# A two-layer graph network on one core: earlier weight loads, batch-norm constants per chunk, norm steps two tiles apart, and a split range check

## The chip, the cores and the metric

The kernel runs on one core of a Trainium2 chip. The metric is the device time of one execution in microseconds (us). The kernel before took 2859.97 us (median of 3 runs, 2859.72 to 2862.34).

Engines are named as in the profile: PE is the matrix engine, PEld its weight load, DVE the vector engine, ACT the scalar engine, POOL is GpSimd, SP issues the DMA transfers. SBUF and PSUM are the two memories on the chip that the kernel works in; PE's results stand in PSUM, from where DVE or ACT reads them.

## The reference, cut to what matters

```python
# x: 16 x 1024 x 256, adj: 1024 x 1024, all float32
def layer0(features, A, W1, b1, g1, be1, W2, b2, g2, be2):
    agg = einsum('nm,bmd->bnd', normalised(A), features)
    h = relu(batchnorm(agg @ W1.T + b1, g1, be1))      # statistics over all 16384 rows
    return batchnorm(h @ W2.T + b2, g2, be2)           # again over all rows

def layer1(x, para, adj, kv_w):
    c = mean(x, channels)                              # per node
    A_s = 1 - abs(2 * sigmoid(c_j - c_i) - 1)          # simplified here
    g = relu(einsum('bcn,bnm->bcm', x.T, adj * A_s) * para)   # the queries
    k, v = split(x @ kv_w)
    return softmax_attention(g, k, v, heads=4)

x = layernorm(x + layer0(x, adj, ...))
x = layernorm(x + layer1(x, para, adj, kv_w))
```

Two points of the reference make seams. Each batch norm needs the statistics of every row before its first output exists. And layer 1 works batch by batch, so its first batch has nothing to overlap with but the end of layer 0.

## The kernel before

The kernel has three parts: layer 0 up to the hidden layer (`pa`, `ph` in the profile), the second half of layer 0 (`po`, in 32 units of 512 rows), and layer 1, a pipeline of 16 batches with 16 steps each. Every step issues score matmuls (`s`), exponentials (`e`), attention matmuls (`o`), and whatever tasks a table puts into it. A chunk is 128 of the channels of a layer: the hidden layer has four (`f`), `po` has two (`c`). A pass is one PE instruction of the profile; one with 512 columns takes 0.43 us from start to start.

```python
        def bn_affine(st, n, g, be, bias, s, t, add_bias, name):
            mv = w0.tile([P, n, 2], F32, name=f"mv_{name}")
            for c in range(n):
                nc.vector.bn_aggr(mv[:, c, :], st[:, c].rearrange("p k s -> p (k s)"))
            # ... six more small DVE operations, and the root on GpSimd, over all n chunks at once
        # ... hidden layer: ACT copies ph, DVE takes its statistics
        bn_affine(st1, HT, g1t, be1t, b1t, s1, t1, True, "bn1")

            def second(u):
                # ...
                for c in range(CT):
                    p = ps.tile([P, FB], F32, tag="a", name="po")
                    for k in range(HT):
                        nc.tensor.matmul(
                            p, W2T[:, k, ts(c, P)], hT[u][:, k, :], start=(k == 0), stop=(k == HT - 1)
                        )
                    nc.vector.tensor_scalar(y[:, c, :], p, b2t[:, c : c + 1], None, op0=OP.add)
                    nc.vector.bn_stats(st2[:, c, b * NH + h, :], y[:, c, :])
                nc.sync.dma_start(yT_dram[b][:, :, ts(h, FB)], y)
        # ...
        bn_affine(st2, CT, g2t, be2t, None, s2, t2, False, "bn2")
```

The tasks of layer 1 that matter here: `load` fetches a tile of 128 rows, `bn2` applies the second batch norm to it, `ln1_a` transposes it (`py`), adds x and takes statistics, `ln1_b` applies the layer norm and sums the row, `x1_t` transposes the result (`px`), `crow` scales the row means `cs` and spreads them over partitions (`pc`), `wg_a` and `wg_b` make the graph weights, `graph` makes the queries (`pg`, then two DVE operations on `qT`), `finish_a` and `finish_b` end a tile.

```python
        def bn2(b, j):
            for c in range(CT):
                t = yts[b, j][:, c, :]
                nc.vector.tensor_scalar(t, t, s2[:, c : c + 1], t2[:, c : c + 1], op0=OP.mult, op1=OP.add)
        def ln1_b(b, j):
            r = x1s[b, j]
            ln_apply(r, r, *mvs.pop((b, j)))                 # DVE, waits for GpSimd's root
            nc.vector.tensor_reduce(css[b][:, j : j + 1], r, AX.X, OP.add)
        def crow(b):
            nc.vector.tensor_scalar_mul(css[b], css[b], 1.0 / C)
            # ... eight transposes of css into PSUM (pc), two ACT copies
        # ...
            for j in range(NT):
                put(b - 2, 3 + j, load, b, j)
                put(b - 2, 4 + j, bn2, b, j)
                put(b - 2, 5 + j, ln1_a, b, j)
                put(b - 2, 6 + j, ln1_b, b, j)
                put(b - 2, 7 + j, x1_t, b, j)
            put(b - 2, 7 + NT, crow, b)
        # ...
            if g == load_weights_at:       # in the first step that loads a tile, after its task list
                load_weights()             # kvw, adj, para: 5.5 MB, on the same queue as the tiles
    fast()
    # then: a range check of all softmax sums, whose flag can start a slow general version
```

## Time and profile before

| view | number |
|---|---|
| span of the profiled run | 2855.9 us |
| PE busy | 2751.3 us (96%) |
| DVE, ACT, POOL busy | 53%, 41%, 13% |
| one batch of layer 1 | 115.08 us |
| last `po` to first `pk` (start to start) | 46.7 us |
| last `o` matmul to the end | 23.5 us |

The main views of this profile stand in the prediction below. One more is the timeline of the tail. Its columns are start, duration, engine, source line, operation, output and inputs, then in brackets the engine's idle time just before it and who ended it.

```profile
2835.43 0.18 DVE L518 RECIPROCAL RD<-pf 128x4 f32<-128x4 f32 x1 [2.16 <-PE pf L516]
2838.53 0.17 DVE L518 RECIPROCAL RD<-pf 128x4 f32<-128x4 f32 x1
...
2849.92 0.14 DVE L606 TENSOR_SCALAR badi<-bad 1x1 int32<-1x1 f32 x1
```

Each of the last four tiles starts with a reciprocal, and these stand 3.1 us apart. The flag of the range check (`badi`) is ready 14.6 us after the first of them.

### The profile page before, as it was taken

How to read it: one execution, taken by the hardware profiler on the slowest of the kernel's cores; microseconds unless marked ns; L12 is line 12 of the kernel's file. 1: busy time of each engine (PE TensorE's matmuls, PEld its weight loads, DVE VectorE, ACT ScalarE, POOL GpSimd, SP SyncE). 2: the span in 40 equal slices, each digit the busy share in tenths (PEclk: the TensorE clock that was granted, in tenths of full speed). 3: DMA queues.
4: the chain of work that ended last, by engine and by line, in shares of the span. 5: the costliest groups of instructions: out<-in, count | busy, mean ns of one | idle time of the engine just before them, and what ended most of it. 6: DMA issues, size and time to landing. Idle time of an engine off the chain costs nothing.

```text
span 2855.9 us, 25725 instructions
## 1 busy us (share of the span) xinstructions
PE 2751.3 (96%) x9426; PEld 1170.7 (41%) x9426; DVE 1502.2 (53%) x2717; ACT 1162.0 (41%) x1487; POOL 377.5 (13%) x523
## 2 busy tenths in 40 slices
PE   7999999999899599999999999999999999999997
PEld 5444444444344244434434344344343443434332
DVE  3011111012444457667686686776766857668556
ACT  1111111112741155645546455364464553644633
POOL 0000000000000112122121221221212212113012
PEclk7999999999999699999999999999999999999998
DMA  3121122120463410001010010010100100101000
GB/s 104 59 88 59 74 88 78 70 103 0 158 232 111 151 30 25 28 19 39 19 32 30 16 43 24 23 35 18 38 30 15 41 20 29 34 13 43 8 10 22
DMA packets 109988, 146.97 MB, mean 51 GB/s; under 512 B 10272, under 2 KB 92704, under 8 KB 103712
## 3 DMA queue, kind: packets, MB, share of 16 engines
q1 hardware_dynamic: 109856, 145.27, 14.9%
q8 instruction: 76, 1.25, 0.2%
q14 instruction: 56, 0.46, 0.1%
HBM read 86.52 MB, written 58.72 MB: 51 GB/s over the span
## 4 chain that ended last, share of the span: by engine, by line
PE 96%; DVE 2%; DMA 1%; POOL 0%; ACT 0%; issue 0%; SPq 0%; POOLq 0%; ACTq 0%
PE s L455 17%; PE o L485 17%; PE pg L435 16%; PE pa L201 15%; PE po L264 8%; PE ph L214 8%; PE pk L408 4%; PE pv L419 4%; PE pf L515 2%; PE pd L504 1%; PE py L364 1%; PE px L377 1%; PE pd L172 1%; PE pc L388 1%; PE pf L516 0%; DMA yt<-yT 0%
## 5 line engine op out<-in xcount | busy, mean ns | idle before, releaser
L467 ACT ACTIVATE e<-s 128x1024 f32<-128x1024 f32 x512 | 496.5, 1022 | 480.7 <-PE s L455 479.4
L455 PE MATMUL s<-qT,kT 64*128 64x512 f32 x2048 | 508.7, 615 | 0.0
L485 PE MATMUL o<-e,v 128*64 128x512 f32 x2048 | 495.7, 605 | 0.0
L476 DVE TENSOR_TENSOR acc<-acc,e 128x1024 f32<-128x1024 f32 x384 | 468.7, 1221 | 41.7 <-ACT e L467 27.8
L435 PE MATMUL pg<-wg,x 128*128 128x512 f32 x1024 | 477.2, 604 | 0.2 <-ACT x1T L378 0.2
L201 PE MATMUL pa<-AhT,x 128*128 128x512 f32 x1024 | 441.9, 592 | 0.0
L233 DVE BATCH_NORM_STATS2 st<-ph 128x6 f32<-128x512 f32 x128 | 89.4, 699 | 570.4 <-ACT hT L232 570.4
L455 PEld LDWEIGHTS s<-qT,kT 64*128 64x128 f32 x2048 | 176.2, 186 | 327.0 <-issue 286.8
L201 PEld LDWEIGHTS pa<-AhT,x 128*128 128x128 f32 x1024 | 194.5, 190 | 244.4 <-issue 244.2
L435 PEld LDWEIGHTS pg<-wg,x 128*128 128x128 f32 x1024 | 182.2, 190 | 240.3 <-issue 219.8
L400 DVE SCALAR_TENSOR_TENSOR wg<-wg,adj_sb 128x1024 f32<-128x1024 f32 x128 | 156.8, 1225 | 227.2 <-ACT wg L396 227.2
L214 PE MATMUL ph<-agg,W1T 128*128 128x512 f32 x512 | 222.2, 592 | 0.0
L485 PEld LDWEIGHTS o<-e,v 128*64 128x64 f32 x2048 | 124.3, 136 | 225.4 <-issue 212.5
L208 ACT COPY agg<-pa 128x512 f32<-128x512 f32 x64 | 37.5, 586 | 402.3 <-PE pa L201 402.3
L68 POOL TENSOR_TENSOR rs_a<-rs_a,mhalf 128x1 f32<-128x1 f32 x128 | 195.9, 1530 | 10.6
L378 ACT COPY x1T<-px 128x256 f32<-128x256 f32 x128 | 47.4, 370 | 357.5 <-PE px L377 357.5
L66 POOL TENSOR_SCALAR rs_z<-mv_z 128x1 f32<-128x1 f32 x128 | 40.8, 319 | 1000.2 <-DVE mv_z L313 1000.2
L264 PE MATMUL po<-hL,W2T 128*128 128x512 f32 x384 | 165.0, 592 | 0.0
L214 PEld LDWEIGHTS ph<-agg,W1T 128*128 128x128 f32 x512 | 97.3, 190 | 122.5 <-issue 122.5
L395 ACT ACTIVATE wg<-crow,cs 128x1024 f32<-128x1024 f32 x128 | 147.0, 1149 | 0.0
L396 ACT ACTIVATE wg<-wg 128x1024 f32<-128x1024 f32 x128 | 135.3, 1057 | 4.1
L232 ACT COPY hT<-ph 128x512 f32<-128x512 f32 x128 | 75.0, 586 | 144.7 <-PE ph L214 144.7
(97 smaller groups left out, 2229.5 us busy)
## 6 DMA issues: line engine op xcount, KB each, us to landing
h<-hT SPq DMA_DIRECT2D x24, 1024.0 KB, 3.8
hL<-h SPq DMA_DIRECT2D x24, 1024.0 KB, 6.2
x<-in_x_dram SPq DMA_DIRECT2D x16, 1024.0 KB, 5.5
yT<-y SPq DMA_DIRECT2D x32, 512.0 KB, 3.6
yt<-yT SPq DMA_DIRECT2D x128, 128.0 KB, 2.6
xr<-in_x_dram SPq DMA_DIRECT2D x128, 128.0 KB, 2.3
out_dram<-r SPq DMA_DIRECT2D x128, 128.0 KB, 1.7
A<-in_adj_dram SPq DMA_DIRECT2D x4, 1024.0 KB, 8.1
```

Of the source, the lines that this page charges most:

```text
L68: nc.gpsimd.tensor_tensor(dst, src, mhalf[:, :n], OP.pow)
L201: nc.tensor.matmul(p, xts[b][:, k, ts(c, P)], AhT[:, k, ts(h, FB)], start=(k == 0), stop=(k == NT - 1),)
L214: nc.tensor.matmul(p, W1T[:, k, ts(f, P)], aggT[b][:, k, ts(h, FB)], start=(k == 0), stop=(k == CT - 1),)
L264: nc.tensor.matmul(p, W2T[:, k, ts(c, P)], hT[u][:, k, :], start=(k == 0), stop=(k == HT - 1))
L395: nc.scalar.activation(t, crows[b], AF.Abs, bias=css[b][:, i : i + 1], scale=-1.0)
L396: nc.scalar.activation(t, t, AF.Tanh, scale=-0.5)
L400: nc.vector.scalar_tensor_tensor(t, t, 1.0, adj_sb[:, i, :], op0=OP.add, op1=OP.mult)
L435: nc.tensor.matmul(pg[b], x1s[b, k][:, ts(c, P)], wgs[b, k][:, ts(h, FB)], start=(k == 0), stop=(k == NT - 1))
L455: nc.tensor.matmul(t[:, h, :], kTs[b, pair][h * HD : (h + 1) * HD, ts(cb, P)], qTs[b, pair][h * HD : (h + 1) * HD, ts(hf, FB)], start=True ...
L467: nc.scalar.activation(E[g, a], S.pop((g, a)), AF.Exp)
L476: nc.vector.tensor_add(ACC[b, hf, pair], ACC[b, hf, pair], E[g, a])
L485: nc.tensor.matmul(O[b, hf, pair][h * HD : (h + 1) * HD, :], vs[b][:, cb, pair * P + h * HD : pair * P + (h + 1) * HD], E[g, a][:, h, :], ...
```

## The change

The intent is to shorten the places where PE stands idle: the two seams of layer 0, the short wait in each batch, and the tail. The diff, cut to its core (left out, among other things: `reuse_waits="tile"` for the PSUM buffers of `po`, more small buffers in layer 1, and `finish_b` of the last four tiles one step later):

```diff
-        def bn_affine(st, n, g, be, bias, s, t, add_bias, name):
+        def bn_affine(st, c, g, be, bias, s, t, name):          # one chunk c
+            nc.vector.bn_aggr(mv, st[:, c].rearrange("p k s -> p (k s)"))
+            rsqrt(rs, mv[:, 1:2], EPS)                          # GpSimd
+            nc.vector.tensor_add(mu, mv[:, 0:1], bias[:, col])
+            nc.vector.tensor_sub(mu, bias[:, col], mu)
+            nc.vector.tensor_mul(s[:, col], rs, g[:, col])
+            nc.vector.scalar_tensor_tensor(t[:, col], mu, s[:, col], be[:, col], op0=OP.mult, op1=OP.add)
@@ hidden layer, after each chunk's statistics
+                            if u == len(units) - 1:
+                                bn_affine(st1, f, g1t, be1t, b1t, s1, t1, "bn1")
@@ second(u)
+                if u == order[0]:
+                    mm.sort(key=lambda ck: ck[1])               # by chunk of the hidden layer
-                    nc.vector.tensor_scalar(y[:, c, :], p, b2t[:, c : c + 1], None, op0=OP.add)
-                    nc.vector.bn_stats(st2[:, c, b * NH + h, :], y[:, c, :])
+                    nc.vector.bn_stats(st2[:, c, b * NH + h, :], po[c])
+                    nc.scalar.copy(y[:, c, :], po[c])
+                    if u == order[-1]:
+                        bn_affine(st2, c, g2t, be2t, b2t, s2, t2, "bn2")
@@ loop over the units (the buffers of layer 1 now lie on the right side of SBUF)
+                if k == KEEP:
+                    load_weights()
+                if k == len(units) - 2:
+                    for j in range(LDP):
+                        load(0, j)
@@ layer 1
-                nc.vector.tensor_scalar(t, t, s2[:, c : c + 1], t2[:, c : c + 1], op0=OP.mult, op1=OP.add)
+                nc.scalar.activation(t, t, AF.Identity, bias=t2[:, c : c + 1], scale=s2[:, c : c + 1])
@@ ln1_b: apply and row sum in one DVE operation
-            ln_apply(r, r, *mvs.pop((b, j)))
-            nc.vector.tensor_reduce(css[b][:, j : j + 1], r, AX.X, OP.add)
+            nc.vector.scalar_tensor_tensor(r, r, mv[:, 0:1], rs.to_broadcast([P, C]),
+                op0=OP.subtract, op1=OP.mult, accum_out=css[b][:, j : j + 1])
@@ wg_a, for odd i
+                nc.scalar.activation(t, crows[b], AF.Tanh, bias=hcs[b][:, i : i + 1], scale=-0.5)
+                nc.vector.tensor_scalar(ti, ti, -(2**31), None, op0=OP.bitwise_or)
@@ finish_b, on ACT, with a product from GpSimd
-            ln_apply(r, r, *mr)
+            nc.scalar.activation(r, r, AF.Identity, bias=nm, scale=rs)
@@ the table
-                put(b - 2, 6 + j, ln1_b, b, j)
-                put(b - 2, 7 + j, x1_t, b, j)
+                put(b - 2, 7 + j, ln1_b, b, j)
+                put(b - 2, 8 + j, x1_t, b, j)
+        put(B - 1, NS // NH, range_so_far)          # the first 120 of 128 tiles
+        put(B - 1, NS + FB // P, range_all)         # the last 8, right after their reciprocals
```

More of the change, by code (lines that the diff above doesn't have):

```diff
@@ L79, in gnn_norm_attention_kernel @@
     yT_dram = [yT_all[b] for b in range(B)]
+    LDP = 3
     s2 = const.tile([P, CT], F32, name="s2")
@@ L96, in gnn_norm_attention_kernel @@
         aggT = []
-        def bn_affine(st, n, g, be, bias, s, t, add_bias, name):
-            mv = w0.tile([P, n, 2], F32, name=f"mv_{name}")
-            for c in range(n):
-                nc.vector.bn_aggr(mv[:, c, :], st[:, c].rearrange("p k s -> p (k s)"))
-            mu = w0.tile([P, n], F32, name=f"mu_{name}")
-            if add_bias:
-                nc.vector.tensor_add(mu, mv[:, :, 0], bias)
-                nc.vector.tensor_sub(mu, bias, mu)
-            else:
-                nc.vector.tensor_scalar_mul(mu, mv[:, :, 0], -1.0)
-            var = w0.tile([P, n], F32, name=f"var_{name}")
-            nc.vector.tensor_copy(var, mv[:, :, 1])
-            rs = w0.tile([P, n], F32, name=f"rs_{name}")
-            rsqrt(rs, var, EPS)
-            nc.vector.tensor_mul(s, rs, g)
-            nc.vector.tensor_mul(mu, mu, s)
-            nc.vector.tensor_add(t, mu, be)
+        def bn_affine(st, c, g, be, bias, s, t, name):
+            col = slice(c, c + 1)
+            mv = w0.tile([P, 2], F32, name=f"mv_{name}{c}")
+            nc.vector.bn_aggr(mv, st[:, c].rearrange("p k s -> p (k s)"))
+            rs = w0.tile([P, 1], F32, name=f"rs_{name}{c}")
+            rsqrt(rs, mv[:, 1:2], EPS)
+            mu = w0.tile([P, 1], F32, name=f"mu_{name}{c}")
+            nc.vector.tensor_add(mu, mv[:, 0:1], bias[:, col])
+            nc.vector.tensor_sub(mu, bias[:, col], mu)
+            nc.vector.tensor_mul(s[:, col], rs, g[:, col])
+            nc.vector.scalar_tensor_tensor(t[:, col], mu, s[:, col], be[:, col], op0=OP.mult, op1=OP.add)
+        s1 = w0.tile([P, HT], F32, name="s1")
+        t1 = w0.tile([P, HT], F32, name="t1")
         with ExitStack() as ph1:
@@ L233, in gnn_norm_attention_kernel, with load_weights, load @@
                             nc.vector.bn_stats(st1[:, f, u, :], p)
+                            if u == len(units) - 1:
+                                bn_affine(st1, f, g1t, be1t, b1t, s1, t1, "bn1")
                         if u < len(units) - KEEP:
                             nc.sync.dma_start(h_dram[u], hT.pop(u))
-        s1 = w0.tile([P, HT], F32, name="s1")
-        t1 = w0.tile([P, HT], F32, name="t1")
-        bn_affine(st1, HT, g1t, be1t, b1t, s1, t1, True, "bn1")
+        right = lambda name, bufs: ctx.enter_context(tc.tile_pool(name=name, bufs=bufs, side="right"))
+        keep = right("keep", 1)
+        ldp = right("ldp", LDP)
+        RD = keep.tile([P, B * NT + 1, HEADS], F32, name="RD")
+        ones32 = keep.tile([P, 32], F32, name="ones32")
+        nc.gpsimd.memset(ones32, 1.0)
+        kvw = keep.tile([P, CT, 2 * C], F32, name="kvw")
+        para_sb = keep.tile([P, CT, N], F32, name="para_sb")
+        adj_sb = keep.tile([P, NT, N], F32, name="adj_sb")
+        yts, xrs = {}, {}
+        def load_weights():
+            nc.sync.dma_start(kvw, kv_w.rearrange("(c p) f -> p c f", p=P))
+            for i in range(0, NT, 2):
+                nc.sync.dma_start(
+                    adj_sb[:, i : i + 2, :], adj[i * P : (i + 2) * P, :].rearrange("(c p) m -> p c m", p=P)
+                )
+            nc.sync.dma_start(para_sb, para.rearrange("o (c p) h w -> p c (o h w)", p=P))
+        def load(b, j):
+            yts[b, j] = ldp.tile([P, CT, P], F32, tag="yt", name=f"yt{b}_{j}")
+            nc.sync.dma_start(yts[b, j], yT_dram[b][:, :, ts(j, P)])
+            xrs[b, j] = ldp.tile([P, C], F32, tag="xr", name=f"xr{b}_{j}")
+            nc.sync.dma_start(xrs[b, j], x[b, ts(j, P), :])
         with ExitStack() as ph2:
             yp = ph2.enter_context(tc.tile_pool(name="yp", bufs=3))
-            ps = ph2.enter_context(tc.tile_pool(name="ps2", bufs=4, space=PSUM))
+            ps = ph2.enter_context(tc.tile_pool(name="ps2", bufs=4, space=PSUM, reuse_waits="tile"))
             order = list(range(len(units) - KEEP, len(units))) + list(range(len(units) - KEEP))
@@ L260, in second @@
                 y = yp.tile([P, CT, FB], F32, tag="y", name=f"y{u}")
-                for c in range(CT):
-                    p = ps.tile([P, FB], F32, tag="a", name="po")
-                    for k in range(HT):
-                        nc.tensor.matmul(
-                            p, W2T[:, k, ts(c, P)], hT[u][:, k, :], start=(k == 0), stop=(k == HT - 1)
-                        )
-                    nc.vector.tensor_scalar(y[:, c, :], p, b2t[:, c : c + 1], None, op0=OP.add)
-                    nc.vector.bn_stats(st2[:, c, b * NH + h, :], y[:, c, :])
+                po = [ps.tile([P, FB], F32, tag="a", name="po") for c in range(CT)]
+                mm = [(c, k) for c in range(CT) for k in range(HT)]
+                if u == order[0]:
+                    mm.sort(key=lambda ck: ck[1])
+                for c, k in mm:
+                    nc.tensor.matmul(
+                        po[c], W2T[:, k, ts(c, P)], hT[u][:, k, :], start=(k == 0), stop=(k == HT - 1)
+                    )
+                for c in range(CT):
+                    nc.vector.bn_stats(st2[:, c, b * NH + h, :], po[c])
+                    nc.scalar.copy(y[:, c, :], po[c])
+                    if u == order[-1]:
+                        bn_affine(st2, c, g2t, be2t, b2t, s2, t2, "bn2")
                 nc.sync.dma_start(yT_dram[b][:, :, ts(h, FB)], y)
@@ L281, in gnn_norm_attention_kernel @@
                         fetch(order[KEEP + AHEAD + k - 1])
-        bn_affine(st2, CT, g2t, be2t, None, s2, t2, False, "bn2")
+                if k == KEEP:
[3 more added lines that the diff above has]
+                        load(0, j)
     NP = HEADS // 2
     den_lo, den_hi = 1e-20, 1e30
-    keep = ctx.enter_context(tc.tile_pool(name="keep", bufs=1))
-    RD = keep.tile([P, B * NT, HEADS], F32, name="RD")
-    ones32 = keep.tile([P, 32], F32, name="ones32")
-    nc.vector.memset(ones32, 1.0)
-    ones64 = None
-    kvw = keep.tile([P, CT, 2 * C], F32, name="kvw")
-    para_sb = keep.tile([P, CT, N], F32, name="para_sb")
-    adj_sb = keep.tile([P, NT, N], F32, name="adj_sb")
-    def load_weights():
-        nc.sync.dma_start(kvw, kv_w.rearrange("(c p) f -> p c f", p=P))
-        for i in range(0, NT, 2):
-            nc.sync.dma_start(
-                adj_sb[:, i : i + 2, :], adj[i * P : (i + 2) * P, :].rearrange("(c p) m -> p c m", p=P)
-            )
-        nc.sync.dma_start(para_sb, para.rearrange("o (c p) h w -> p c (o h w)", p=P))
     def ln_stats(sm, r, name):
@@ L323, in fast @@
         pool = lambda name, bufs, **k: fx.enter_context(tc.tile_pool(name=name, bufs=bufs, **k))
-        ldp = pool("ldp", 3)
         x1p = pool("x1p", 21)
@@ L334, in fast @@
         otp = pool("otp", 3)
-        sm = pool("sm", 4)
+        sm = pool("sm", 6)
         rp = pool("rp", 4)
@@ L339, in fast @@
         ps_t = pool("ps_t", 3, space=PSUM)
-        yts, xrs, x1s, x1Ts, css, crows, mvs, wgs = {}, {}, {}, {}, {}, {}, {}, {}
+        x1s, x1Ts, css, crows, mvs, wgs = {}, {}, {}, {}, {}, {}
         kTs, qTs, vs, S, E, ACC, O, OT, DT = {}, {}, {}, {}, {}, {}, {}, {}, {}
-        pg = {}
-        def load(b, j):
-            yts[b, j] = ldp.tile([P, CT, P], F32, tag="yt", name=f"yt{b}_{j}")
-            nc.sync.dma_start(yts[b, j], yT_dram[b][:, :, ts(j, P)])
-            xrs[b, j] = ldp.tile([P, C], F32, tag="xr", name=f"xr{b}_{j}")
-            nc.sync.dma_start(xrs[b, j], x[b, ts(j, P), :])
+        pg, hcs = {}, {}
         def bn2(b, j):
@@ L370, in ln1_b @@
             r = x1s[b, j]
-            ln_apply(r, r, *mvs.pop((b, j)))
-            nc.vector.tensor_reduce(css[b][:, j : j + 1], r, AX.X, OP.add)
+            mv, rs = mvs.pop((b, j))
+            nc.vector.scalar_tensor_tensor(
+                r,
+                r,
+                mv[:, 0:1],
+                rs.to_broadcast([P, C]),
+                op0=OP.subtract,
+                op1=OP.mult,
+                accum_out=css[b][:, j : j + 1],
+            )
         def x1_t(b, j):
@@ L382, in crow @@
             nc.vector.tensor_scalar_mul(css[b], css[b], 1.0 / C)
+            hcs[b] = sm.tile([P, NT], F32, tag="hcs", name=f"hcs_{b}")
+            nc.vector.tensor_scalar_mul(hcs[b], css[b], 0.5)
             crows[b] = crp.tile([P, N], F32, tag="crow", name=f"crow_{b}")
@@ L394, in wg_a @@
             wgs[b, i] = t
-            nc.scalar.activation(t, crows[b], AF.Abs, bias=css[b][:, i : i + 1], scale=-1.0)
-            nc.scalar.activation(t, t, AF.Tanh, scale=-0.5)
+            if i % 2:
+                nc.scalar.activation(t, crows[b], AF.Tanh, bias=hcs[b][:, i : i + 1], scale=-0.5)
+                ti = t.bitcast(mybir.dt.int32)
+                nc.vector.tensor_scalar(ti, ti, -(2**31), None, op0=OP.bitwise_or)
+            else:
+                nc.scalar.activation(t, crows[b], AF.Abs, bias=css[b][:, i : i + 1], scale=-1.0)
+                nc.scalar.activation(t, t, AF.Tanh, scale=-0.5)
         def wg_b(b, i):
@@ L525, in finish_a, with range_so_far, range_all @@
             nc.vector.tensor_add(r, r, x1s.pop((b, i)))
-            R[b, i] = (r, ln_stats(sm, r, f"z{b}_{i}"))
+            mv, rs = ln_stats(sm, r, f"z{b}_{i}")
+            nm = sm.tile([P, 1], F32, tag="nm", name=f"nm_{b}_{i}")
+            nc.gpsimd.tensor_scalar(nm, mv[:, 0:1], rs, -1.0, op0=OP.mult, op1=OP.mult)
+            R[b, i] = (r, rs, nm)
         def finish_b(b, i):
-            r, mr = R.pop((b, i))
-            ln_apply(r, r, *mr)
+            r, rs, nm = R.pop((b, i))
+            nc.scalar.activation(r, r, AF.Identity, bias=nm, scale=rs)
             nc.sync.dma_start(out[b, ts(i, P), :], r)
+        last = (B - 1) * NT
+        def range_so_far():
+            flat = RD[:, :last, :].rearrange("p a h -> p (a h)")
+            for k, op in enumerate((OP.max, OP.max, OP.min, OP.min)):
+                if k % 2 == 0:
+                    nc.vector.tensor_reduce(RD[:, B * NT, k : k + 1], flat, AX.X, op)
+                else:
+                    nc.vector.tensor_copy(RD[:, B * NT, k : k + 1], RD[:, B * NT, k - 1 : k])
+        badi = []
+        def range_all():
+            flat = RD[:, last:, :].rearrange("p a h -> p (a h)")
+            mm = sm.tile([P, 4], F32, tag="mm", bufs=1, name="mm")
+            nc.vector.tensor_reduce(mm[:, 0:1], flat, AX.X, OP.max)
+            nc.vector.tensor_reduce(mm[:, 1:2], flat, AX.X, OP.min)
+            nc.vector.tensor_scalar(mm[:, 2:3], mm[:, 0:1], 1.0 / den_lo, None, op0=OP.is_le)
+            nc.vector.tensor_scalar(mm[:, 3:4], mm[:, 1:2], 1.0 / den_hi, None, op0=OP.is_ge)
+            pf = ps_t.tile([P, FB], F32, tag="t", name="pflag")
+            nc.tensor.matmul(pf[:1, :2], ones, mm[:, 2:4], start=True, stop=True)
+            bad = sm.tile([1, 2], F32, tag="bad", bufs=1, name="bad")
+            nc.vector.tensor_scalar(bad, pf[:1, :2], -1.0, float(P), op0=OP.mult, op1=OP.add)
+            badi.append(keep.tile([1, 1], mybir.dt.int32, name="badi"))
+            nc.vector.tensor_add(badi[0], bad[:, 0:1], bad[:, 1:2])
         NS = NT // 2 * NP * NH
@@ L543, in fast @@
             for j in range(NT):
-                put(b - 2, 3 + j, load, b, j)
+                if b > 0 or j >= LDP:
+                    put(b - 2, 3 + j, load, b, j)
                 put(b - 2, 4 + j, bn2, b, j)
                 put(b - 2, 5 + j, ln1_a, b, j)
-                put(b - 2, 6 + j, ln1_b, b, j)
-                put(b - 2, 7 + j, x1_t, b, j)
+                put(b - 2, 7 + j, ln1_b, b, j)
+                put(b - 2, 8 + j, x1_t, b, j)
             put(b - 2, 7 + NT, crow, b)
@@ L568, in fast @@
                 put(b, s + 1 + i % (FB // P), finish_a, b, i)
-                put(b, s + 2 + i % (FB // P), finish_b, b, i)
-        last = max(at)
+                put(b, s + 2 + i % (FB // P) + (b == B - 1 and hf == NH - 1), finish_b, b, i)
+        put(B - 1, NS // NH, range_so_far)
+        put(B - 1, NS + FB // P, range_all)
         nsteps = B * NS
-        load_weights_at = -2 * NS + 3
-        for g in range(min(at), max(last, nsteps - 1) + 1):
+        for g in range(min(at), max(max(at), nsteps - 1) + 1):
             if 0 <= g + 1 < nsteps:
@@ L581, in fast @@
                 f(*a)
-            if g == load_weights_at:
-                load_weights()
             if 0 <= g < nsteps:
                 attend(g)
-    fast()
-    with ExitStack() as cx:
-        sm = cx.enter_context(tc.tile_pool(name="smc", bufs=1))
-        psc = cx.enter_context(tc.tile_pool(name="psc", bufs=1, space=PSUM))
-        flat = RD.rearrange("p a h -> p (a h)")
-        mm = sm.tile([P, 4], F32, name="mm")
-        nc.vector.tensor_reduce(mm[:, 0:1], flat, AX.X, OP.max)
-        nc.vector.tensor_reduce(mm[:, 1:2], flat, AX.X, OP.min)
-        nc.vector.tensor_scalar(mm[:, 2:3], mm[:, 0:1], 1.0 / den_lo, None, op0=OP.is_le)
-        nc.vector.tensor_scalar(mm[:, 3:4], mm[:, 1:2], 1.0 / den_hi, None, op0=OP.is_ge)
-        pf = psc.tile([1, 2], F32, name="pflag")
-        nc.tensor.matmul(pf, ones, mm[:, 2:4], start=True, stop=True)
-        fl = sm.tile([1, 2], F32, name="fl")
-        nc.vector.tensor_copy(fl, pf)
-        bad = sm.tile([1, 1], F32, name="bad")
-        nc.vector.tensor_add(bad, fl[:, 0:1], fl[:, 1:2])
-        badi = sm.tile([1, 1], mybir.dt.int32, name="badi")
-        nc.vector.tensor_scalar(badi, bad, -1.0, 2.0 * P, op0=OP.mult, op1=OP.add)
-        flag = nc.values_load(badi[0:1, 0:1], min_val=0, max_val=2 * P, skip_runtime_bounds_check_because="a count of up to 256")
+        return nc.values_load(
+            badi[0][0:1, 0:1],
+            min_val=0,
+            max_val=2 * P,
+            skip_runtime_bounds_check_because="a count of up to 256",
+        )
+    flag = fast()
     def general(b):
```

## The prediction

> **What bounds the kernel now.** I read the page first: the busy shares, the slices, the chain of work that ended last.
>
> ```profile
> PE   7999999999899599999999999999999999999997
> PEclk7999999999999699999999999999999999999998
> PE 96%; DVE 2%; DMA 1%; POOL 0%; ACT 0%; issue 0%; SPq 0%; POOLq 0%; ACTq 0%
> ```
>
> TensorE (PE) is the bound: 96% of the chain, nines in nearly all slices (one slice is 2855.9/40 = 71.4 us). The holes are slice 1 (start), 11 (714 to 785 us, the seam between the two halves of layer 0), 14 (928 to 1000 us, the seam between the layers) and 40 (tail). The change removes no matmul, so all it can win is PE idle time: 2855.9 - 2751.3 busy = 104.6 us. The view of waits, for PE, says who holds it; columns are total us, times, longest us.
>
> ```profile
> PE py L364 <- DVE yt L355: 26.0, 6, 16.3
> PE pc L388 <- DVE cs L382: 20.0, 15, 1.4
> PE pw L161 <- DMA w1n<-in_L_gnn_W_dram: 15.1, 1, 15.1
> PE pflag L600 <- DVE mm L598: 12.6, 1, 12.6
> PE po L264 <- ACT hT L254: 8.4, 1, 8.4
> PE px L377 <- DVE x L319: 5.4, 7, 2.1
> PE py L364 <- ACT wg L395: 3.2, 1, 3.2
> ```
>
> The w1n wait is the start, which the change leaves alone. The others are four places: seam A (8.4), seam B (26.0 + 5.4 + 3.2), one 1.3 us wait in each later batch (20.0), the tail (12.6 and what follows). A gain of 2% is 57 us, over half of all idle PE time. I then read the timeline at each place.
>
> ```profile
> 717.55 0.59 ACT L232 COPY hT<-ph 128x512 f32<-128x512 f32 x1 [1.13 <-PE ph L214]
> 718.17 0.70 DVE L233 BATCH_NORM_STATS2 st<-ph 128x6 f32<-128x512 f32 x1 [1.02 <-ACT hT L232]
> 718.79 3.65 DVE L103 BATCH_NORM_AGGREGATE mv_bn<-st 128x2 f32<-128x192 f32 x4
> 725.04 20.54 ACT L254 ACTIVATE hT<-hT,t,s 128x512 f32<-128x512 f32 x29 [6.90 <-DVE t L116]
> ...
> 953.39 2.16 SPq L303 DMA_DIRECT2D adj_sb<-in_adj_dram  x4
> 955.60 0.56 SPq L306 DMA_DIRECT2D para_sb<-in_L_gnn_para_dram  x1
> 970.09 0.60 DVE L355 TENSOR_SCALAR yt<-yt,s,t 128x128 f32<-128x128 f32 x2 [14.79 <-DMA yt<-yT]
> 993.69 7.96 PE L408 MATMUL pk<-x1T,kvw 128*128 128x512 f32 x16
> ...
> 1850.94 0.16 DVE L382 TENSOR_SCALAR cs<-cs 128x8 f32<-128x8 f32 x1
> 1851.15 1.09 PE L388 MATMUL pc<-ident,cs 128*128 128x128 f32 x8 [1.32 <-DVE cs L382]
> ```
>
> Columns: start, duration, engine, instruction, then the idle time before it and its releaser. Seam A: PE ends at 717.5 and waits while DVE aggregates four chunks in a row and GpSimd takes the root. Seam B: the weights of layer 1 are issued ahead of the second tile's load, whose normalisation waits 14.79 us; then eight tiles go through at 2.87 us each (971 to 991 us), and the first large matmul (pk) starts 46.2 us after layer 0 ended (947.5). Steady batch: after the last pg matmul PE waits 1.32 us for DVE.
>
> **What the Trainium skill says.** "TensorE: Matmul & The Clock Gate", Part 1, says the array falls to half rate after an idle window of about 3.4 us and recovers after as much sustained work. The trace agrees: after the 8.39 us gap the first weight loads stand 0.86 us apart, later ones 0.43; so a gap that shrinks can also win some 1.7 us of slow matmuls. "PSUM — Partial Sum Buffer", "PSUM bank collisions raise a hardware error", has two engines' accesses to one bank serialised, reads included: above, the statistics start 0.03 us after ACT's copy ended, so both readers of a result run in turn. "ScalarE: Activation LUTs", "Table sets", puts identity, relu and abs into every set, and exp with tanh into one; the trace has one table load in the run (1.3 us), and I expect no more. "DMA: Bandwidth & Descriptors", anatomy section, gives a fixed cost of about 2.0 us to each transfer; here a 128 KB tile takes 2.6 us to land.
>
> **The change part by part.**
>
> Seam A (constants per chunk). DVE's serial work per chunk is now statistics 0.70 + aggregate 0.91 + a GpSimd round trip (gaps 0.2, 0.23, root of one column 0.57: about 1.0) + two small steps 0.4 = 3.05 us. The first statistics of the last unit are at about 713.0, so chunk 3 is ready at 713.0 + 4 x 3.05 = 725.2, no earlier than the 724.94 of before; DVE waiting for GpSimd in order eats the overlap. But chunks 0 to 2 are ready at 716, 719 and 722, and the first unit's matmuls are sorted by chunk, so three quarters of that unit is done while chunk 3 is made. Its activation (0.80) and last 4 matmuls (0.43 each) end near 727.8; before, the unit ended at 734.7. At full clock that is 7 us, with those four cold 5. **I take 6.**
>
> The y half of layer 0. DVE loses the 0.75 us bias addition, ACT gains two PSUM copies of 0.59 per unit. A unit is 16 matmuls x 0.43 = 6.86 us of PE; ACT has 4 activations (2.93 together) plus 1.2. ACT can no longer run ten units ahead, but needs only one. No effect.
>
> Weights early. 5.5 MB took some 16 us of DMA in seam B (953 to 970). They now go after unit 8, where DMA is 67 to 70% busy, PE-paced, and h tiles are fetched up to 12 units ahead; hidden. Tiles 0 to 2 of layer 1 are also loaded before the seam.
>
> Seam B, from the end T of the last po matmul: statistics, one aggregate, GpSimd and two steps end at T+3.2 (chunk 0 done before), the normalisation is now two ACT instructions, py and the addition follow: first addition at T+4.3 (before T+6.7). Then tiles at DVE's pace: addition 0.45 + statistics 0.46 + aggregate 0.18 + one fused apply-and-sum 0.46 with its accumulator read 0.08, about 1.6 us, with no GpSimd wait as the second step comes two tiles later. A load ring of 3 buffers gives (2.6 + 0.7 + 0.9)/3 = 1.4, so DVE still sets it. The eighth addition is at T+15.5, its apply at T+17.6, and pk 2.6 us later (before 2.95, less the reduction): T+20.2. **26 us saved.** In the next stretch ACT bound the wg tiles (1.15 + 1.06 us each, 8 of them); four lose an instruction, but two bn2 activations per tile now stand in ACT's queue too. The first py of batch 1 comes about 17.3 after pk instead of 18.05, the eighth wg tile 1.7 earlier. **I take 1.5.**
>
> Steady batches. 115.0 us each, PE busy 113.75. The x1 transposes (0.38 us of PE) move one step later, between the last pg matmul and pc: they fill 0.38 of the 1.32. The chain pg, two DVE operations, cs is otherwise unchanged. 15 x 0.38 = **5.7 us**. DVE sheds bn2 (16 x 0.29), the reduction (8 x 0.42) and the final apply (8 x 0.41), and gains four integer ORs; ACT gains about what it loses. DVE was 80 and ACT 59 of 115 us, so neither matters.
>
> Tail. Before: four tiles at 3.1 us each, because DVE waits for GpSimd, then 2.2 us of range check over 512 numbers, then 5.8 us to the end of the span. After: 1.76 us per tile (no wait, the apply on ACT), then a check over 36 numbers of 1.4 us. 4 x 1.34 + 0.8 = **6 us**, if the 5.8 us follows the flag and not the last store, which now ends about 2 us after it.
>
> Sum: 6 + 26 + 1.5 + 5.7 + 6 = 45.2 us; 2860 - 45 = about 2814 us.
>
> **Rivals.** (1) ACT becomes the seam's bound: bn2 and wg share its queue in order. Against: 0.7 us of bn2 plus a 0.37 copy per tile is under 1.6. If it held, seam B would give 20, the time 2820. (2) The weights or the y stores fall behind: y has 3 buffers, 20.6 us of room, and a store queued behind 5.5 MB waits some 16 to 19 us. If that stalled PE once, 5 us lost. (3) The 1.3 us wait per batch goes wholly, if DVE gets there earlier: 14 us more, 2800. Against: in the trace DVE idles 6.7 us before the two qT operations, so PE, not DVE load, times that chain. (4) The transfers of the seam were hidden anyway: no, the 14.79 us wait has PE idle 16.3.
>
> **Range and chances.** Largest uncertainties: tile pace (1.4 to 2.1 us, 5 us in all), seam A's clock (2), the tail (2), new waits in 15 batches (each 0.1 us is 1.5). I give 2804 to 2826. Over 2% needs 57 us, 12 beyond my sum, with rival 3 or all parts at their best: 0.1. Slower over 2%: 0.01.
>
> **What would show it.** Right: no wait of DVE for a yt load at the seam, pk about 20 us after the last po; tiles there 1.6 us apart; the pc wait 0.94 x 15 = 14 us; tail from last o matmul to the end 17 us instead of 23; batches 114.6 us long; a first unit of seam A ending 10 us after the last ph. Wrong: PE waits on ACT yt in every batch, a second table load, po waiting on hL or y, or pc waits near zero.

## The result, and the profile after

The changed kernel took 2817.44 us (median of 4 runs, 2816.89 to 2818.15), the kernel before on the same chip 2861.15 us (4 runs). The ratio is 0.9847 (95% interval 0.983 to 0.9864). A ratio here is the mean time of one kernel's fast runs over that of the other's of the same rounds, so it isn't quite the ratio of the medians. A change of less than 2% is called "same" here, as was forecast, and 2817 lies in the forecast range.

The busy share of PE in 40 slices, and the PE waits of the changed kernel (total us, times, longest us):

```profile
PE   7999999999999899999999999999999999999998
```

```profile
PE pc L405 <- DVE cs L397: 18.0, 15, 1.2
PE pflag L580 <- DVE mm L578: 6.2, 1, 6.2
PE py L371 <- ACT yt L362: 5.4, 3, 2.0
PE px L392 <- DVE x L379: 3.7, 7, 1.1
PE po L288 <- ACT hT L276: 3.2, 3, 1.4
```

The hole at slice 11 is closed, that at slice 14 is shallow. The 26.0 us wait for a normalised tile is 5.4 us, the wait at the first seam 3.2 instead of 8.4, the tail's 6.2 instead of 12.6. The wait before `pc` has hardly moved: 18.0 instead of 20.0 us.

To see where the time went I cut both traces at the same instructions, from start to start (the starts are read to 0.1 us, so a difference can be off by 0.1):

| stretch | before | after | gained | predicted |
|---|---|---|---|---|
| start to first `pa` | 58.2 | 62.4 | -4.2 | 0 |
| first `pa` to last `ph` | 658.7 | 658.7 | 0 | 0 |
| last `ph` to last `po` (seam A) | 230.1 | 223.8 | 6.3 | 6 |
| last `po` to first `pk` (seam B) | 46.7 | 19.4 | 27.3 | 26 |
| first `pk` to first `s` | 49.8 | 47.7 | 2.1 | 1.5 |
| first `s` to last `o` (batches) | 1788.9 | 1786.8 | 2.1 | 5.7 |
| last `o` to the end (tail) | 23.5 | 17.6 | 5.9 | 6 |
| sum without the start | 2797.7 | 2754.0 | 43.7 | 45.2 |

The start is not the change's; that is shown in the first experiment. Without it the traces differ by 43.7 us. That the medians differ by 43.7 us too is partly chance, as each timed run has an early or a late start.

**Seam A** in the timeline of the changed kernel:

```profile
722.25 0.81 ACT L276 ACTIVATE hT<-hT,t,s 128x512 f32<-128x512 f32 x1
...
729.42 0.22 DVE L111 SCALAR_TENSOR_TENSOR t<-mu_bn,s,be1t 128x1 f32<-128x1 f32 x1
730.60 14.86 PE L288 MATMUL po<-hT,W2T 128*128 128x512 f32 x34 [1.09 <-ACT hT L276]
```

Chunk 0 is activated at 722.25, 0.5 us after the last `ph` matmul ended (721.7). The last chunk's constants are ready at 729.6. Four passes of 0.43 us later, at 732.3, the first unit is done: 10.6 us after the last `ph`, against 17.2 before.

**Seam B**, two successive tiles of the kernel before, then the changed kernel:

```profile
974.28 0.41 DVE L366 TENSOR_TENSOR x<-py,xr 128x256 f32<-128x256 f32 x1
977.15 0.41 DVE L366 TENSOR_TENSOR x<-py,xr 128x256 f32<-128x256 f32 x1
```

```profile
945.49 0.70 DVE L292 BATCH_NORM_STATS2 st<-po 128x6 f32<-128x512 f32 x1 [0.27 <-PE po L288]
949.60 0.42 DVE L373 TENSOR_TENSOR x<-py,xr 128x256 f32<-128x256 f32 x1 [0.94 <-PE py L371]
...
956.02 0.18 DVE L327 BATCH_NORM_AGGREGATE mv_a<-st_a 128x2 f32<-128x6 f32 x1
956.12 0.45 DVE L379 SCALAR_TENSOR_TENSOR x<-x,mv_a,rs_a 128x256 f32<-128x256 f32 x1
956.49 0.09 DVE L379 DVE_READ_ACCUMULATOR x<-x,mv_a,rs_a 128x1 f32 x1
956.49 0.42 DVE L373 TENSOR_TENSOR x<-py,xr 128x256 f32<-128x256 f32 x1
...
959.28 0.42 DVE L373 TENSOR_TENSOR x<-py,xr 128x256 f32<-128x256 f32 x1
964.32 8.20 PE L431 MATMUL pk<-x1T,kvw 128*128 128x512 f32 x16
```

Layer 0 ends at 945.45. The first addition of layer 1 comes 4.15 us later, the eighth 9.7 us after that, so a tile takes 1.38 us (before: 2.87). The first `pk` starts 18.9 us after the end of layer 0, against 46.1.

**One batch**: two pairs of transposes in a stream, then the work around `pc`:

```profile
1002.90 0.38 PE L392 MATMUL px<-ident,x 128*128 128x128 f32 x2
1003.12 0.38 PE L371 MATMUL py<-ident,yt 128*128 128x128 f32 x2
...
1817.07 0.38 PE L392 MATMUL px<-ident,x 128*128 128x128 f32 x2
1818.34 0.16 DVE L397 TENSOR_SCALAR cs<-cs 128x8 f32<-128x8 f32 x1
1818.65 1.06 PE L405 MATMUL pc<-ident,cs 128*128 128x128 f32 x8 [1.20 <-DVE cs L397]
```

The transposes do stand in the gap now, but PE still waits 1.20 us, where the prediction had 0.94.

**The tail**:

```profile
2801.41 0.18 DVE L541 RECIPROCAL RD<-pf 128x4 f32<-128x4 f32 x1 [2.79 <-PE pf L539]
2803.18 0.15 DVE L541 RECIPROCAL RD<-pf 128x4 f32<-128x4 f32 x1
...
2809.38 0.15 DVE L584 TENSOR_TENSOR badi<-bad 1x1 int32<-1x1 f32 x1
```

The tiles come 1.75 us apart and the flag is ready 8.1 us after the first reciprocal. From the flag to the end of the span it is 6.9 us (before: 5.8), so in this pair one microsecond of the gain was given back. The last tile's apply on ACT starts only at 2809.89, after the flag; that this is the reason is argued, not shown, as the stretch lies between 6.1 and 7.1 us in the other profiles with this apply.

### The profile page after: what moved, and what is told of

It is laid out like the page before. It is cut to its first block, busy times and chain, and to the rows that moved or that the text cites. A ratio compares the mean times of both kernels' runs of the same rounds, so it can differ in the third digit from the quotient of the medians.

```text
span 2816.4 us, 26243 instructions
## 1 busy us (share of the span) xinstructions
PE 2750.9 (98%) x9426; PEld 1174.2 (42%) x9426; DVE 1352.6 (48%) x2364; ACT 1295.2 (46%) x1871; POOL 498.2 (18%) x660
## 4 chain that ended last, share of the span: by engine, by line
PE 96%; DVE 2%; DMA 0%; ACT 0%; issue 0%; POOL 0%; SPq 0%; DVEq 0%; POOLq 0%; ACTq 0%
PE s L478 17%; PE o L508 17%; PE pg L458 16%; PE pa L199 16%; PE po L288 8%; PE ph L212 8%; PE pk L431 4%; PE pv L442 4%; PE pf L538 2%; PE pd L527 1%; PE py L371 1%; PE pd L170 1%; PE px L392 1%; PE pc L405 1%; PE pf L539 0%; DMA w1n<-in_L_gnn_W_dram 0%
## 5 line engine op out<-in xcount | busy, mean ns | idle before, releaser
L66 POOL TENSOR_SCALAR rs_z<-mv_z 128x1 f32<-128x1 f32 x128 | 52.2, 408 | 900.3 <-DVE mv_z L327 884.4
L66 POOL TENSOR_SCALAR rs_a<-mv_a 128x1 f32<-128x1 f32 x128 | 124.8, 975 | 435.8 <-DVE mv_a L327 435.7
L68 POOL TENSOR_TENSOR rs_a<-rs_a,mhalf 128x1 f32<-128x1 f32 x128 | 157.9, 1234 | 10.7
L393 ACT COPY x1T<-px 128x256 f32<-128x256 f32 x128 | 47.7, 372 | 239.9 <-PE px L392 239.9
```

Of the source, the lines that this page charges most:

```text
L66: nc.gpsimd.tensor_scalar(dst, src, add, None, op0=OP.add)
L68: nc.gpsimd.tensor_tensor(dst, src, mhalf[:, :n], OP.pow)
```

## The experiments

Twelve kernels ran, all correct. Their times scatter by 4 to 5 us for a reason that has nothing to do with them (the first experiment), so beside each median I give the span of the profiled run less its start. It agrees to 0.2 us in the two profiles of the kernel before. Seam A (223.7) and the batches (1786.7) repeat to 0.1 us in every kernel that doesn't touch them. Seam B (19.4 to 20.2), the stretch from `pk` to `s` (47.1 to 48.2) and the tail (17.0 to 18.0) scatter by about 1 us, so a smaller difference there is not read as the edit's.

| run | median us | ratio to before | span less start | seam A | seam B | pk to s | batches | tail |
|---|---|---|---|---|---|---|---|---|
| before | 2861.15 | 1 | 2797.7 | 230.1 | 46.7 | 49.8 | 1788.9 | 23.5 |
| changed | 2817.44 | 0.9847 | 2754.0 | 223.8 | 19.4 | 47.7 | 1786.8 | 17.6 |
| e9_before_again | 2859.57 | 0.9998 | 2797.9 | 230.0 | 46.6 | 49.7 | 1789.0 | 23.8 |
| e1_weights_alone | 2845.06 | 0.9947 | 2783.7 | 230.0 | 32.4 | 50.1 | 1788.9 | 23.5 |
| e2_weights_late | 2832.04 | 0.9897 | 2768.2 | 223.7 | 33.8 | 47.2 | 1786.7 | 18.0 |
| e3_one_apart | 2827.26 | 0.9883 | 2767.7 | 223.7 | 27.3 | 51.3 | 1788.8 | 17.8 |
| e4_scale_early | 2797.43 | 0.9778 | 2736.8 | 223.7 | 19.8 | 47.5 | 1769.6 | 17.4 |
| e5_constants_whole | 2825.00 | 0.9873 | 2763.0 | 230.3 | 21.6 | 48.2 | 1786.7 | 17.4 |
| e6_no_sort | 2819.68 | 0.9859 | 2758.3 | 228.2 | 19.6 | 47.1 | 1786.8 | 17.8 |
| e7_bn2_on_dve | 2822.14 | 0.9868 | 2759.8 | 223.7 | 25.2 | 48.4 | 1786.7 | 17.0 |
| e8_tail_dve | 2820.40 | 0.9861 | 2758.3 | 223.7 | 20.2 | 47.4 | 1786.7 | 21.5 |
| e11_wg_two_steps | 2816.54 | 0.9845 | 2756.3 | 223.7 | 19.9 | 49.3 | 1786.7 | 17.9 |
| e12_hcs_gpsimd | 2814.16 | 0.9840 | 2754.0 | 223.7 | 20.0 | 47.5 | 1786.7 | 17.3 |
| e10_best | 2795.86 | 0.9778 | 2735.3 | 221.5 | 19.7 | 48.1 | 1769.5 | 17.7 |

### e9_before_again: is the later start the change's?

The edit is none: the kernel before, once more.

> The kernel before, unchanged, to see how much of the 4.2 us later start of the changed kernel's profile is the run's own. Theory (the clock of the 128 one-column matmuls at the start differs from run to run): the first aggregation matmul may start near 58 us or near 62 us, and the span less that start is 2797.7 +- 1 us again. Rival (the change made the start slower): 58.2 us again here, and 62.4 us in every kernel derived from the changed one. Time 2860 +- 3 us.

Its own profile again had the early start. But the kernels derived from the changed one, whose start is untouched, fell on both sides. Here the start's 128 one-column matmuls in the changed kernel, and in e12_hcs_gpsimd:

```profile
18.70 27.31 PE L170 MATMUL pd<-ones,A 128*128 128x1 f32 x128
```

```profile
18.59 24.21 PE L170 MATMUL pd<-ones,A 128*128 128x1 f32 x128
```

Of fourteen profiles ten took 24.2 to 24.4 us and four 27.3 us (the changed kernel, e2, e4, e5). So the rival falls: it is the run's own, and the profiles before and after happened to fall on different sides. The timed runs of the kernel before show two levels too. The mean clock that the profiler reports as granted to PE tells the side: in this run 2857.74 and 2857.45 us came with 0.982, 2861.50 and 2861.40 us with 0.987. All four runs of the changed kernel have 0.995, the clock of its late start, so its median is that of the slower side, and a median of a derived kernel can lie some microseconds below it for that reason alone. What decides the side stays open.

### e1_weights_alone and e2_weights_late: were the transfers of the seam hidden?

e1 is the kernel before with this part alone, e2 the changed kernel without it:

```diff
# e1, on the kernel before           # e2, on the changed kernel
+                if k == KEEP:        -                if k == KEEP:
+                    load_weights()   -                    load_weights()
+                if k == len(units) - 2:
+                    for j in range(3):     + if g == 4 - 2 * NS:   # after tile 0's bn2
+                        load(0, j)         +     load_weights()
```

> Kernel before plus only the early weights and the three early tile loads. Theory: the 16.3 us PE wait for the second tile falls under 2 us, the seam from the last po matmul to the first pk matmul goes from 46.1 to about 31 us, the second half of layer 0 keeps its 230 us, time 2860 - 15 = 2845 us. Rival (the transfer only moves its cost: h tiles or y stores stall in layer 0, or the tiles are slow for another reason): po waits on hL or ACT appear, or the seam stays over 40 us; time over 2853 us.

> Changed kernel with the weights issued after layer 0 again, but behind the three early tile loads. Theory: the 5.5 MB take 16 us of DMA from about T (end of the last po matmul), tile 3 lands near T+18 instead of T+7, so the seam grows from 18.9 to about 31 us and the time from 2817 to 2829 us. Rival (three early tiles alone cover the transfer): seam under 22 us, time under 2821 us.

The longest PE waits for a normalised tile, in e1 and in e2:

```profile
PE py L370 <- DVE yt L361: 11.9, 7, 5.7
```

```profile
PE py L369 <- ACT yt L360: 19.1, 4, 13.7
```

Alone, the early weights gave 14.0 us (2797.7 to 2783.7), all of it in seam B; layer 0 kept its 230.0 us. Taken out of the changed kernel they cost 14.2 us, two more than expected, and a 13.7 us wait is back. So the transfer was not hidden before, it is hidden now, and three early tiles don't cover it. In e1 the tiles still come 2.87 us apart: that half of the seam belongs to other parts.

### e3_one_apart: the two norm steps of a tile

```diff
-                put(b - 2, 7 + j, ln1_b, b, j)
-                put(b - 2, 8 + j, x1_t, b, j)
+                put(b - 2, 6 + j, ln1_b, b, j)
+                put(b - 2, 7 + j, x1_t, b, j)
```

> Changed kernel with the two norm steps of a tile one step apart again (apply at 6+j, transposes at 7+j). Theory: at the seam DVE waits for GpSimd in each tile again, so tiles come about 1.9 to 2.0 us apart instead of 1.39 (+4 us), and the batches return from 114.92 to 115.08 us (+2.3 us in all, pc wait from 18 to 20 us): time 2817 + 6 = 2823 us. Rival (tile pace set by the load ring or by ACT): pace stays 1.4, time 2819 to 2820 us.

It cost 13.7 us, more than twice what I expected (the medians say 9.8, the changed kernel's being that of the late start). Two successive applies on DVE at the seam:

```profile
952.37 0.48 DVE L379 SCALAR_TENSOR_TENSOR x<-x,mv_a,rs_a 128x256 f32<-128x256 f32 x1 [0.99 <-POOL rs_a L68]
...
954.87 0.48 DVE L379 SCALAR_TENSOR_TENSOR x<-x,mv_a,rs_a 128x256 f32<-128x256 f32 x1 [0.99 <-POOL rs_a L68]
```

Tiles come 2.50 us apart: DVE's work of 1.4 us and the whole round trip to GpSimd, 0.99 us, of which I had counted half. That is 7.9 us in seam B. Another 3.6 us came in the next stretch: PE waited 2.06 us for a graph weight instead of 1.27 and then ran six `pg` passes in 4.54 us instead of 2.84; the recorded clock is 0.50 over most of them, and 1.00 there in the changed kernel. The batches lost 2.0 us, and their `pc` wait was 20.0 again: the distance between the steps is what the batches had gained.

### e7_bn2_on_dve: which engine sets the pace of the seam?

```diff
-                nc.scalar.activation(t, t, AF.Identity, bias=t2[:, c : c + 1], scale=s2[:, c : c + 1])
+                nc.vector.tensor_scalar(t, t, s2[:, c : c + 1], t2[:, c : c + 1], op0=OP.mult, op1=OP.add)
```

> Changed kernel with the second batch-norm's apply on DVE again. Theory: DVE sets the tile pace at the seam, so 0.57 us more per tile, from 1.39 to about 1.97 us, +4.5 us from po to pk; the 2.0 us wait of the first py of batch 1 for ACT shrinks by some 1 us; batches within 0.3 us of 114.92 as PE bounds them: time 2817 + 3.5 = 2820.5 us. Rival (ACT or the load ring sets the pace): pace within 0.2 of 1.39, time under 2818.5 us.

```profile
951.13 0.42 DVE L373 TENSOR_TENSOR x<-py,xr 128x256 f32<-128x256 f32 x1 [0.17 <-PE py L371]
953.30 0.42 DVE L373 TENSOR_TENSOR x<-py,xr 128x256 f32<-128x256 f32 x1 [0.17 <-PE py L371]
```

The tiles come 2.16 us apart, 0.78 more than in the changed kernel: the 0.57 of the two operations, and 0.17 in which DVE now also waits for the transpose. Seam B lost 5.8 us. DVE sets the pace, and the first rival of the prediction (ACT becomes the seam's bound) falls. The move pays although the work costs more on ACT: a pair of these operations takes 0.88 us there and 0.57 us on DVE. One expectation missed: the wait of batch 1's first `py` didn't shrink by 1 us, it grew from 2.0 to 2.65.

### e5_constants_whole and e6_no_sort: seam A

e5 computes both sets of constants for all chunks at once, as before, after the loops. e6 only takes the sort away:

```diff
-                if u == order[0]:
-                    mm.sort(key=lambda ck: ck[1])
```

> Changed kernel with both sets of batch-norm constants computed for all chunks at once again. Theory: from the last ph to the last po matmul 230 us instead of 223.8 (+6), and from the last po to the first pk about 1.3 us more, the second aggregate: time 2817 + 7.5 = 2825 us. Rival (the seam-A gain came from the y half, ACT copies in place of the DVE addition): 224 us stays, time under 2820 us.

> Changed kernel with the first unit's matmuls in their old order. Theory: after the last chunk is ready 10 matmul passes are left instead of 4, 6 x 0.43 = 2.6 us more from the last ph to the last po matmul: 2820 us. Rival (the chunks alone give the gain): under 0.5 us more.

e5 lost 6.5 us in seam A and 2.2 in seam B, 9.0 in all: the chunks carry the gain, not the work moved from DVE to ACT. e6 lost 4.4 us, two thirds of seam A's gain, where I had expected 2.6. Its trace shows why: after the last chunk it has ten passes left, and PE's weight loads stand 0.86 us apart in the first five of them, 0.43 after; in the changed kernel they stand 0.43 apart. The recorded clock falls to 0.50 from 724.3 to about 731.2 us in e6 and stays at 1.00 in the changed kernel. The sort wins twice: fewer passes after the last chunk, and a PE that kept its clock.

### e8_tail_dve: the tail

```diff
-            nc.gpsimd.tensor_scalar(nm, mv[:, 0:1], rs, -1.0, op0=OP.mult, op1=OP.mult)
-            nc.scalar.activation(r, r, AF.Identity, bias=nm, scale=rs)
+            ln_apply(r, r, mv, rs)          # DVE, and finish_b one step later as before
```

> Changed kernel with the last apply on DVE again, one step after its statistics, and without the product for ACT on GpSimd. Theory: the four last tiles come 3.1 us apart again instead of 1.75, so the tail from the last o matmul to the end grows by about 4.5 us, from 17.6 to 22 us, the batches stay 114.92 us: time 2822 us. Rival (the tail was the range check's): tail under 18.7 us, time under 2819 us.

The reciprocals of the last tiles stand at 2797.75, 2800.85, 2803.95 and 2807.05: 3.1 us apart again. The tail grew by 3.9 us to 21.5. Of the tail's 5.9 us, the apply on ACT thus carries about two thirds. The range check was not tried alone, but this run against the kernel before shows its part: with tiles equally far apart, the flag comes 12.1 us after the first of these reciprocals instead of 14.6.

### e11_wg_two_steps: one activation less for every other graph weight

```diff
-            if i % 2:
+            if False:
```

> Changed kernel with abs and tanh for every wg tile, as before. Theory: ACT has 4 x 1.1 us more in the stretch after the first pk, where PE waits 2.0 us for a normalised tile and 1.3 us for a wg tile, so from the first pk to the first s 50 to 51 us instead of 47.7; batches unchanged: time 2820 us. Rival (the stretch is bound by PE): 48 us or less, time 2817.5 us.

The stretch from first `pk` to first `s` grew by 1.6 us, in the expected direction at half the size. Among kernels that don't touch this stretch it lies between 47.1 and 48.2 us, so 49.3 is little outside that, and the times can't tell (2816.54 us, three of four runs with the early start, against 2817.44). I call it inconclusive: at most 2 us.

### e4_scale_early: the wait in every batch

The wait that the change left nearly whole is a chain: the last `pg` matmul, two DVE operations on `qT` (0.69 and 0.43 us), then the scaling of `cs`, which needs none of them and only stands behind them in DVE's queue.

```diff
+        def cscale(b):
+            nc.vector.tensor_scalar_mul(css[b], css[b], 1.0 / C)
+            # ... and hcs, both taken out of crow
+            put(b - 2, 6 + NT, cscale, b)
             put(b - 2, 7 + NT, crow, b)
```

> Changed kernel with only the two small DVE scalings of cs moved one step earlier, ahead of the two qT operations in DVE's queue. Theory (the wait before pc is the DVE chain pg, qT, qT, cs, and the moved transposes fill little of it): the pc wait falls from 18.0 us to under 5 us in all, a batch from 114.92 to about 114.0 us, time 2817 - 15 = 2802 us. Rival (PE waits for a PSUM slot or for something else there): the wait stays over 12 us under another name, time over 2812 us.

The line of `pc` is gone from the list of waits. One batch takes 113.77 us; busy time in a stretch of 114 us:

```profile
1692.00:1806.00 114.00, 113.97 (x452) 46.34 (x448) 73.84 (x130) 65.54 (x93) 31.42 (x40) 1.00 0.09 28
```

The columns after the stretch are its length and the busy us of PE, PEld, DVE, ACT and POOL. PE is idle for 0.03 us. The batches gained 17.2 us (1786.8 to 1769.6), the theory's 15 and a little more, and no other wait took the place of this one. Two moved lines brought over a third of what the whole change had.

### e12_hcs_gpsimd: why does pc start later after cs?

In the changed kernel `pc` starts 0.15 us after the scaling of `cs` ended (1818.50 to 1818.65), in the kernel before 0.05 us.

```diff
-            nc.vector.tensor_scalar_mul(hcs[b], css[b], 0.5)
+            nc.gpsimd.tensor_scalar(hcs[b], css[b], 0.5, None, op0=OP.mult)
```

> Changed kernel with the halved cs made on GpSimd, not DVE. It asks why pc starts 0.15 us after cs ended, against 0.05 us before. Theory A (the second small DVE operation delays the signal): pc wait from 18.0 to about 16.5 us in all, batches 114.82 us. Theory B (it is PE's second wait, for a PSUM buffer freed by ACT): 18.0 us again. Time 2816 or 2817.5 us, too close to tell by time alone.

The wait is 18.0 us again and the batches 1786.7, so the second small DVE operation is not the reason. The trace puts PE's weight load for `pc` down to ACT's copy of `px` as well, which fits a second wait, for a PSUM buffer; that is argued, not shown. The lower median of this run, 2814.16, is the start again: three of its four runs have the clock of the early one.

### e10_best: both improvements

e4_scale_early, and in addition the constants of a chunk in two halves. The half that needs GpSimd's root is issued after the next chunk's statistics:

```diff
                             nc.vector.bn_stats(st1[:, f, u, :], p)
                             if u == len(units) - 1:
-                                bn_affine(st1, f, g1t, be1t, b1t, s1, t1, "bn1")
+                                if f > 0:
+                                    bn_tail(f - 1, g1t, be1t, s1, t1, "bn1")
+                                bn_head(st1, f, b1t, "bn1")     # aggregate, root, mean
+                                if f == HT - 1:
+                                    bn_tail(f, g1t, be1t, s1, t1, "bn1")
```

> Early scaling of cs as in e4_scale_early, and in the last unit of each half of layer 0 the part of the constants that needs GpSimd's result is issued after the next chunk's statistics, so DVE doesn't wait for GpSimd between chunks. Theory: a chunk takes 2.45 us of DVE instead of 3.08, the last chunk is ready 1.5 us earlier, from the last ph to the last po 222.3 instead of 223.7 us, time 2797.4 - 1.5 = 2796 us; batches 113.77 us as in e4. Rival (the clock or ACT sets the first unit): 223.5 us again, 2797.4 us.

Seam A went from 223.7 to 221.5 us and the `po` wait from 3.2 to 1.4. The time is 2795.86 us, ratio 0.9778 (0.9765 to 0.9792) to the kernel before: clear of 2%, as e4_scale_early was with the same ratio. That it is faster than e4 is shown by seam A alone; the times of the two overlap.

## Why the prediction was right, point by point

- **The bound.** PE idle time was all there was to win, and the sum of the stretches came to 43.7 us of the predicted 45.2. The sum is closer than its worst term: the batches fell 3.6 us short, and seam A, seam B and the stretch after it gave 2.2 more than predicted. No engine took PE's place: in a batch DVE fell from 80 to 74 busy us and ACT rose from 59 to 65, of 115. The table load of ACT stayed the only one (1.28 us, before and after).
- **Seam A**, predicted 6, measured 6.3. The last chunk was indeed no earlier than before (7.9 us after the last `ph`, against 7.4). A chunk took 3.08 us of DVE; the prediction's terms add up to 3.01 where it wrote 3.05, and a single aggregation takes 1.02 us instead of 0.91. Both halves of the argument were tested: without the chunks the gain is gone (e5), without the sort two thirds of it (e6). That DVE waits for GpSimd between chunks was right too: e10 removed the wait and gained 2.2 us.
- **Weights early**, hidden: 14 us alone and 14 us in the whole (e1, e2); `po` never waited for a transfer, so the second rival (weights or y stores fall behind) fell.
- **Seam B**, predicted 26, measured 27.3. First addition 4.15 us after layer 0 (predicted 4.3), tiles 1.38 us apart (1.6), first `pk` after 18.9 (20.2). The tile pace was a little too pessimistic: I had added 0.45, 0.46, 0.18, 0.46 and 0.08. In the trace the operations start 0.46, 0.46, 0.10 and 0.38 us apart: the fused apply starts before the aggregation's record ends, and the next addition starts with the accumulator read (shown above). The single engine and the reason were right: DVE (e7), freed of GpSimd's round trip (e3).
- **The stretch after it**, predicted 1.5, measured 2.1, with the two waits foreseen (2.0 us for a tile behind ACT). e11 leaves its share open.
- **Steady batches**, predicted 5.7, measured 2.1 (114.92 us each instead of 114.6): this is the step that was mis-sized. "They fill 0.38 of the 1.32" took the duration of a pair of transposes for the time that PE gives them. The record of the pair is 0.38 us long, but the next PE instruction starts 0.22 us after it began (in the changed kernel `px` at 1002.90, `py` at 1003.12, shown above). And "otherwise unchanged" missed 0.10 us: `pc` starts 1.42 us after the last `pg` ended instead of 1.32. A wait of 1.32 - 0.22 + 0.10 = 1.20 is what the trace shows. e3 confirms that the move is worth 2.0 us over the batches.
- **The third rival** (the wait goes wholly) was rightly given little weight for this change, because PE times that chain through `pg` and `qT`. e4 shows the other half, which the prediction didn't draw: the scaling had no need to stand in that chain at all.
- **The tail**, predicted 6, measured 5.9, two thirds of it through ACT's apply (e8). The condition I had set, that the last 5.8 us follow the flag alone, wasn't quite met: they became 6.9. What the estimate missed on the other side is that the first reciprocal also came 0.4 us sooner after the last `o`.
- **The expectations** for e3 and e6 were too small (6 and 2.6 us; 13.7 and 4.4 measured): in both, PE stood idle for longer and the recorded clock fell to 0.50, and in e3 the round trip to GpSimd was counted by half.
- **A reading of the PSUM page.** The prediction's "serialised" is right only as something that software adds: in "PSUM — Partial Sum Buffer", "PSUM bank collisions raise a hardware error", the compiler orders such accesses. In the trace, too, DVE's statistics wait for ACT (1.02 us, "<-ACT hT").

## What to carry to other kernels

When PE is busy 96% of the time, list its waits, and for each ask whether the operation at its end really needs the ones ahead of it in its engine's queue; two small operations issued one step earlier were worth 17 us here, while filling the gap with other work was worth 2. At a seam, add up the serial engine's work per tile with the round trips to other engines, and put enough tiles between the two halves of such a trip. Size a move of PE work by the distance to the next instruction's start, not by the recorded duration.

## What the Trainium skill lacked or had wrong

- "TensorE: Matmul & The Clock Gate", Part 4, gives about 275 ns for a transpose of 128 by 128 in bf16. The runs agree for one in float32 (272 to 283 ns), but Part 4 has no spacing for transposes in a stream: a pair of them takes only 0.22 us of PE's time from start to start. That was the prediction's mis-sized step.
- The same page, Part 1, calls the count of slow matmuls run-variable and warns that the trace's clock events can be unreliable. Here the start's 128 one-column matmuls took 24.2 to 24.4 us in ten profiles and 27.3 us in four. The recorded mean clock was 0.54 to 0.57 over that stretch (19 to 46 us) in the short ones and 1.00 in the long ones, so record and pace go opposite ways; the page has no such pair of levels.
- No page has the duration of a power of one column on GpSimd: 0.57 us while DVE was idle or in short operations, 1.59 us beside its long additions.
